# Top-64 routing in the last expert stage: two experts chosen ahead of the weights, and later nodes fetched from DRAM by index

## The chip, the cores and the metric

The kernel runs on one core of a Trainium2 chip. The core has TensorE (PE, with a separate row in the profile for its weight loads, PEld), VectorE (DVE), ScalarE (ACT), GpSimd (POOL) and SyncE (SP), and 16 DMA engines that all its transfers share. SBUF holds the working tiles, PSUM (eight banks here, each 128 x 512 f32) the results of matmuls. The metric is the device time of one execution of the whole program, in microseconds (us); the figure for a kernel is the median over several executions. The data are f32, and a f32 matmul in the source is carried out as two instructions, each with its own weight load; the counts below are of instructions unless they say otherwise.

## The reference

The program is a network of four layers on 512 nodes with 768 features. Each layer adds a graph block and an attention block of the normalized features to `x`, and then a feed-forward block. The change concerns only the feed-forward block of the fourth layer, a mixture of experts in which every *expert* chooses its 64 best nodes:

```python
scores = sigmoid(x @ gate_weight.T)                 # 512 nodes x 16 experts
capacity = ceil(n / E * TOP_K)                      # 512 / 16 * 2 = 64
topk_score, topk_ids = top_k(scores.T, capacity)    # per expert: 64 nodes
xg = x[topk_ids]
gate, up = silu(einsum('ecd,efd->ecf', xg, Wg)), einsum('ecd,efd->ecf', xg, Wu)
out = einsum('ecf,edf->ecd', gate * up, Wd) * topk_score[..., None]
y = zeros((n, d)).at[topk_ids.reshape(-1)].add(out.reshape(-1, d))
return y + silu(x @ Ws_g.T) * (x @ Ws_u.T) @ Ws_d.T # shared expert
```

Here `x` is the layer-normed input, and the result is added to the residual `x`. An expert has a hidden width of 3072; its three matrices are 28.3 MB, those of all sixteen 453 MB. The shared expert has a hidden width of 1536 and sees all nodes.

## The kernel before

**Layout.** Nodes lie in four tiles `t` of 128 (NT = 4, P = 128), features in six chunks of 128 (KC = 6) or two halves of 384 (HW). `xn` is the normalized input with nodes on the partitions, `xnT` the same with features on the partitions. A tile framework lets one write the program in one order; at build time it gives each engine its fixed sequence of instructions, and each instruction its waits on other engines. Nothing is reordered at run time: an instruction that waits holds up all that stands behind it on its engine. PSUM is handed out in banks by `ps` (L222); `copy` (L230) evicts a bank by DVE (L234) and ACT (L236) in turn; `acc` (L310, its matmul is L312) sums products into a bank; `tr` (L317) transposes a block through PE; `to_fm` makes the transposed form of a whole tensor.

**Weights.** `w` (L238) takes one buffer of 128 x 2304 f32 (1152 KB, 1.18 MB) from a pool and has the SP queue load it. In the last stage the pool `f3_w` has ten buffers. SP issues the loads in the order of the program, and each load waits until PE has read the last matmul's operand out of the buffer that it takes over; the loads behind it on SP wait with it. The weights of the shared expert (0.39 MB each) come on POOL's queue into a pool of six.

**Before the stage.** `last_two` (L1398) computes the attention and graph blocks of layer 4. At its end, for each tile `t`, the projection's halves are added to `x` (`add_x`, L360) and `norm1` (L344: statistics L351 and L352, Sqrt on ACT L353, reciprocal L354, the result L355, on DVE) writes the tile of `xn`; after the last tile `to_fm` makes `xnT`, 24 transposes and six copies.

**The seam.** `ffn3` (L1567) first needs its routing:

- *Logits* (L1582 on): for each tile of nodes, the six chunks of `xnT` are the stationary operand and the gate's 16 columns move: 48 matmuls of 16 columns. ACT applies the Sigmoid (L1586) and writes `sc`, nodes by experts.
- *Constants*: two iotas on POOL (L1588, L1590), and `before` (L1593), four 128 x 512 masks by DVE: entry (i, j) of tile t is 1 where node j comes before node 128 t + i.
- *`rank(e)`* (L1597): four transposes of the broadcast column of `sc` put expert e's 512 scores on every partition. For each tile DVE counts the scores that are greater (L1605, 512 columns) and those that are equal and earlier (L1607, 512 columns), each with its sum over the columns; L1609 adds the two. A node's rank is that number, and nodes of rank below 64 are chosen.
- *`choose(g)`* (L1613) compares the ranks of four experts with 0 to 63 (L1616, four instructions of 256 columns): `oh` is one-hot, nodes by slots.
- *`gather(g, f)`*: a matmul of `xn` by `oh` for a chunk f gives the chosen rows of four experts, transposed, in `xg`: 48 instructions of 256 columns for a group of four, and six copies.

Ahead of the first expert matmul stand, in this order on PE, the ranks of experts 0 to 3, `choose(0)`, two matmul pieces of the shared expert (`shared`, L1651; loads L1654, Silu L1661, product L1663), six gathers and the two `shared_down` pieces that belong to them.

**The stream.** Eight pairs q of experts times eight blocks n of 384 hidden units are 64 steps. Step i runs `up` for step i + 1 (L1685: 24 source matmuls in two halves of 64 PE columns, one for each expert of the pair; Silu L1688 on ACT, product L1689 on DVE) and `down` for step i (three transposes, a copy, 12 source matmuls L1701 that accumulate over n in two banks). Its loads are issued as four for `up` of step i + 1 (`up_w`: Wg and Wu of both experts) and two for `down` of step i.

A table `beside` attaches the other work to steps: for g = 1 to 3 the ranks of the next four experts at steps 16(g-1) + 0, 2, 4, 6, `choose(g)` at + 8, the gathers at + 9 to + 14; for each pair, `way` (L1632, one-hot times score, transposed) and four `back` (the outputs of a pair scattered to the nodes by matmul and added to `x`); and the remaining 44 pieces of the shared expert over the first 60 steps. After the last step come four `back` and, for each, the store of a tile of the result by SP (L1758).

An earlier stage already fetches rows by index: a POOL instruction (L828) reads rows of a DRAM copy of the normalized input, `f_there`, into `xb`, and a like DRAM tensor `f_back` is written by ACT's queue.

## Time and profile before

| | us |
|---|---|
| median of three executions (range) | 4346.05 (4344.59 to 4347.77) |
| the profiled execution's own time | 4347.94 |
| its span | 4346.1 |
| PE busy | 4152.7 (96%) |
| PE weight loads | 2128.3 (49%) |
| DVE busy | 1319.1 (30%) |
| ACT busy | 649.5 (15%) |
| POOL busy | 262.9 (6%) |
| mean granted PE clock | 0.984 |
| moved by DMA | 705.98 MB, of it 601.13 MB on SP's weight queue (q1) |

Events in the trace, in us from the start of the span:

| event | us |
|---|---|
| last matmul of the attention projection ends | 3165.7 |
| SP begins to issue the expert weights | 3165.8 |
| last tile of `xn` written | 3169.3 |
| logits begin and end on PE | 3170.4, 3180.2 |
| `sc` written | 3181.8 |
| DVE's ranks of experts 0 to 3 | 3183.1 to 3210.4 |
| gathers on PE | 3210.9 to 3224 |
| first expert matmul (L1685) | 3229.2 |
| first weight load after the first ten is issued | 3233.3 |
| last weight data land | 4331.5 |
| last matmul ends | 4342.1 |

One execution is profiled, so durations come from that one. Busy time is the sum of the durations on an engine, and in this profile the ends of matmuls are modelled: a PE that is busy all the time need not work at its peak. In a row of a group, "busy, mean ns" stands ahead of a bar, and behind it the idle time that the engine had just ahead of these instructions, with what released it. In tables by stretches of time, the number in brackets counts instructions, and the last three columns are the granted PE clock (1 is full), the busy share of the 16 DMA engines and the rate in GB/s.

### The profile page before, as it was taken

Reading aid. Unit: us, or ns where it says so; the run is one execution under the profiler, and the core shown is the slowest. Engines: PE = TensorE matmul, PEld = TensorE weight load, DVE = VectorE, ACT = ScalarE, POOL = GpSimd, SP = SyncE. Lnnn points to the kernel's source line nnn. Section 1 sums busy time; section 2 is a strip of 40 time slices with the busy share of each in tenths; the row PEclk is TensorE's granted clock in tenths of the full one; section 3 lists DMA queues with packets and bytes.
Section 4 is the critical chain, followed back from the end, with each engine's and each line's share of the span. In section 5 each row is a group of like instructions: output and inputs, shape, how many; then the busy total and the mean of one; then the engine's idle time right before and its main releaser. Section 6 shows DMA issues by size and latency. Waiting matters only on the chain. (4 is left out here: it accounts for less than half of the span.)

```text
span 4346.1 us, 40145 instructions
## 1 busy us (share of the span) xinstructions
PE 4152.7 (96%) x16454; PEld 2128.3 (49%) x16454; DVE 1319.1 (30%) x3001; ACT 649.5 (15%) x1235; POOL 262.9 (6%) x307
## 2 busy tenths in 40 slices
PE   7989999999988999999999999988989999999999
PEld 3434555554444566655544444444654444444444
DVE  7772111113332136513221111125842132131111
ACT  1121200002211224411101010013600000000000
POOL 1120000011021010000000000021200000000000
PEclk9999999999999999999999999999989999999999
DMA  3111011121056112211201110072059999999999
GB/s 109 51 61 56 22 44 65 66 73 39 15 211 243 44 51 71 112 38 66 105 33 66 44 66 33 22 288 82 12 220 417 408 419 420 402 420 414 406 409 376
DMA packets 97819, 705.98 MB, mean 162 GB/s; under 512 B 11856, under 2 KB 11920, under 8 KB 28256
## 3 DMA queue, kind: packets, MB, share of 16 engines
q1 hardware_dynamic: 77776, 601.13, 35.0%
q0 software_dynamic: 15952, 91.22, 5.6%
q10 hardware_dynamic: 3904, 11.01, 0.7%
q8 instruction: 133, 2.18, 0.2%
q14 instruction: 54, 0.44, 0.0%
HBM read 682.34 MB, written 20.97 MB: 162 GB/s over the span
## 5 line engine op out<-in xcount | busy, mean ns | idle before, releaser
L1685 PE MATMUL ps<-w,xg 128*64 128x384 f32 x3072 | 569.2, 489 | 3.7 <-DMA w<-in_f_Wu_dram 2.0
L1685 PEld LDWEIGHTS ps<-w,xg 128*64 128x64 f32 x3072 | 233.5, 137 | 296.1 <-issue 273.9
L1356 PE MATMUL ps<-aT,w 128*128 128x512 f32 x864 | 372.3, 592 | 0.0
L1701 PE MATMUL ps<-w,hT 128*64 128x384 f32 x1536 | 326.4, 490 | 3.4 <-DMA w<-in_f_Wd_dram 2.7
L312 PE MATMUL ps<-xnT,w 128*128 128x512 f32 (+1 forms) x732 | 320.9, 595 | 0.2 <-ACT xnT L236 0.2
L1356 PEld LDWEIGHTS ps<-aT,w 128*128 128x128 f32 x864 | 164.2, 190 | 203.6 <-issue 202.3
L360 DVE TENSOR_TENSOR x<-x,ps 128x384 f32<-128x384 f32 x240 | 131.6, 553 | 326.0 <-PE ps L312 256.2
L312 PE MATMUL ps<-w,xnT 128*128 128x384 f32 x672 | 221.7, 486 | 0.2 <-DVE xnT L234 0.2
L312 PEld LDWEIGHTS ps<-xnT,w 128*128 128x128 f32 (+1 forms) x732 | 134.1, 184 | 174.7 <-issue 171.1
L1701 PEld LDWEIGHTS ps<-w,hT 128*64 128x64 f32 x1536 | 133.3, 136 | 168.5 <-issue 146.6
L312 PE MATMUL ps<-w,hT 128*128 128x384 f32 x552 | 187.9, 496 | 8.8 <-ACT hT L850 8.8
L312 PE MATMUL ps<-C,parts 128*128 128x512 bf16 x864 | 188.6, 380 | 2.7 <-DVE inv L1378 2.7
L463 PE MATMUL ps<-ohd,so 128*128 128x512 bf16 x816 | 180.3, 380 | 2.8 <-DVE so L460 2.8
L312 PEld LDWEIGHTS ps<-w,xnT 128*128 128x128 f32 x672 | 127.0, 190 | 88.8 <-issue 4.8
L1366 DVE TENSOR_TENSOR aT<-inv,ps 128x512 f32<-128x512 f32 x72 | 49.5, 687 | 365.6 <-PE ps L312 365.6
L1688 ACT ACTIVATE h<-ps 128x384 f32<-128x384 f32 x64 | 31.4, 491 | 802.5 <-PE ps L1685 802.5
L312 PEld LDWEIGHTS ps<-w,hT 128*128 128x128 f32 x552 | 104.6, 193 | 83.1 <-ACT hT L850 13.4
L1689 DVE TENSOR_TENSOR h<-h,ps 128x384 f32<-128x384 f32 x64 | 35.5, 554 | 348.4 <-PE ps L1685 336.2
L312 PE MATMUL ps<-w,aT 128*128 128x384 f32 (+1 forms) x416 | 139.6, 486 | 0.5 <-DVE aT L234 0.4
L312 PEld LDWEIGHTS <-parts 128*128 128x128 bf16 x864 | 84.8, 98 | 108.1 <-issue 8.8
L312 PE MATMUL ps<-xnT,sw 128*128 128x512 f32 x288 | 136.3, 605 | 0.0
L460 DVE TENSOR_SCALAR so<-io,ind,worth 128x256 bf16<-128x256 int16 x408 | 121.7, 356 | 35.2 <-PE ps L463 35.0
(478 smaller groups left out, 4853.5 us busy)
## 6 DMA issues: line engine op xcount, KB each, us to landing
w<-in_f_Wg_dram SPq DMA_DIRECT2D x128, 1152.0 KB, 12.0
w<-in_f_Wu_dram SPq DMA_DIRECT2D x128, 1152.0 KB, 12.2
w<-in_f_Wd_dram SPq DMA_DIRECT2D x128, 1152.0 KB, 13.2
w<-in_g_w_dram SPq DMA_DIRECT2D x54, 1152.0 KB, 5.1
w<-in_m_wqkv_dram SPq DMA_DIRECT2D x24, 1152.0 KB, 7.2
w<-in_g_t_dram SPq DMA_DIRECT2D x12, 1152.0 KB, 5.4
w<-in_m_wp_dram SPq DMA_DIRECT2D x8, 1152.0 KB, 5.0
ea<-in_edge_attr_dram SPq DMA_DIRECT2D x34, 256.0 KB, 2.7
```

Source lines behind the costliest of these rows:

```text
L312: self.nc.tensor.matmul(out, a, b, start=n == 0, stop=n == len(pairs) - 1)
L360: self.nc.vector.tensor_add(xs, xs, p)
L460: nc.vector.tensor_scalar(so[:, n, :], io[:, h * 256 : (h + 1) * 256], ind[:, 0, j : j + 1], worth[:, n, j : j + 1], OP.is_equal, OP.mult)
L463: nc.tensor.matmul(p, so[:, n, t * P : (t + 1) * P], ohd[:, j, :], start=False, stop=j == (g + 1) * HJ - 1)
L1356: nc.tensor.matmul(outs[nb * 3 + f], w[:, k, f * P : (f + 1) * P], xT[:, k, :], start=first and k == 0, stop=last and k == KC - 1)
L1366: nc.vector.tensor_mul(aT[:, f, :], inv[:, r, :], p)
L1685: nc.tensor.matmul(p[a * 64 : a * 64 + 64, :HW], xg[:, k, e * CAP : (e + 1) * CAP], ws[b][a][:, k, :], start=k == 0, stop=k == KC - 1)
L1688: nc.scalar.activation(h, pg[:, :HW], AF.Silu)
L1689: nc.vector.tensor_mul(h, h, pu[:, :HW])
L1701: nc.tensor.matmul(po[nb][a * 64 : a * 64 + 64, :HW], hT[:, f * P + a * 64 : f * P + a * 64 + 64], wd[a][:, f, nb * HW : (nb + 1) * HW], s ...
```

## The change

Five things change, all in `last_two` and `ffn3`.

1. `last_two` makes a DRAM tensor `f3_there` (512 x 768) and, behind each of the last four `norm1`, has ACT's queue write the tile of `xn` to it. `to_fm` moves from the end of `last_two` into `ffn3`.
2. The set-up in `ffn3` is written ahead of `to_fm` and on POOL; `before` becomes one 128 x 128 mask. A Sigmoid on a constant column is written there too.
3. Logits: the gate's 16 columns are stationary and `xnT` moves, six source matmuls of 512 columns into 16 partitions, then a copy to SBUF and four transposes back to nodes by experts.
4. `rank(e)`: scores in tiles before the node's own are counted with "greater or equal", those in its own and later tiles with "greater", and equality times `before` is needed in the 128 columns of its own tile alone; `tensor_reduce` adds the three counts.
5. Experts are chosen by pairs. Only the pair of the first eight steps is gathered by matmul, and only its two ranks stand ahead of the first expert matmul, with one piece of the shared expert. For each later pair q, `fetch(q)` makes the node number of each slot (`oh` times `number`, a table that holds each node's number in two parts, four source matmuls; a sum and a conversion to an integer on DVE) and has POOL read the 128 rows from `f3_there`; `turn(q)` transposes them (six transposes, two copies). They are attached as ranks at steps 8(q-1) and + 1, `choose` and `fetch` at + 2, `turn` at + 5. The other 47 pieces of the shared expert are spread over the first 60 steps.

```diff
--- before.py
+++ after.py
@@ -1395,10 +1395,11 @@
-    def last_two(self, xn, xnT, out, outT):
+    def last_two(self, xn, xnT, out):
         nc, tc, d = self.nc, self.tc, self.d
+        there = self.dp.tile([N, D], F32, name="f3_there")
         xs = self.chunks(xnT)
@@ -1455,10 +1456,12 @@
                 if over:
                     while len(ready) <= t:
-                        self.norm1(self.x, out, len(ready))
+                        u = len(ready)
+                        self.norm1(self.x, out, u)
+                        nc.scalar.dma_start(there[u * P : (u + 1) * P, :], out[:, u, :])
                         ready.append(t)
             assert over
-        self.to_fm(out, outT)
+        return there
@@ -1564,7 +1567,7 @@
-    def ffn3(self, xn, xnT):
+    def ffn3(self, xn, xnT, there):
@@ -1577,22 +1580,29 @@
             self.cw.close()
             self.wp = c.enter_context(tc.tile_pool(name="f3_w", bufs=10, side="right"))
+            first = self.small.tile([P, 1], F32, name="r3")
+            nc.scalar.activation(first, self.eps, AF.Sigmoid)
+            io = one.tile([P, P], F32, name="io")
+            nc.gpsimd.iota(io, pattern=[[1, P]], base=0, channel_multiplier=0, allow_small_or_imprecise_dtypes=True)
+            number = one.tile([P, NT, 2], F32, name="number")
+            nc.gpsimd.tensor_copy(number, self.number)
+            above = one.tile([P, NT, NX], F32, name="above")
+            counted = one.tile([P, NX, NT, 3], F32, name="counted")
+            nc.gpsimd.memset(counted, 0.0)
+            before = one.tile([P, P], BF16, name="before")
+            nc.gpsimd.tensor_scalar(before, io, self.me, None, OP.is_lt)
+            self.to_fm(xn, xnT)
             gw = self.col("f3_gw", 0, KC * NX).rearrange("p (k e) -> p k e", k=KC)
             p = self.ps()
+            self.acc(p[:NX], [(gw[:, k, :], xnT[:, k, :]) for k in range(KC)])
+            loT = one.tile([NX, N], F32, name="loT")
+            nc.vector.tensor_copy(loT, p[:NX])
+            p = self.ps()
             for t in range(NT):
-                self.acc(p[:, t * NX : (t + 1) * NX],
-                         [(xnT[:, k, t * P : (t + 1) * P], gw[:, k, :]) for k in range(KC)])
+                self.tr(p[:, t * NX : (t + 1) * NX], loT[:, t * P : (t + 1) * P])
             sc = one.tile([P, NT, NX], F32, name="sc")
             nc.scalar.activation(sc, p[:, : NT * NX].rearrange("p (t e) -> p t e", t=NT), AF.Sigmoid)
-            io = one.tile([P, N], F32, name="io")
-            nc.gpsimd.iota(io, pattern=[[1, N]], base=0, channel_multiplier=0, allow_small_or_imprecise_dtypes=True)
-            me = one.tile([P, NT], F32, name="me")
-            nc.gpsimd.iota(me, pattern=[[P, NT]], base=0, channel_multiplier=1, allow_small_or_imprecise_dtypes=True)
-            before = one.tile([P, NT, N], BF16, name="before")
-            for t in range(NT):
-                nc.vector.tensor_scalar(before[:, t, :], io, me[:, t : t + 1], None, OP.is_lt)
-            above = one.tile([P, NT, NX], F32, name="above")
-            equal = one.tile([P, NT, NX], F32, name="equal")
             def rank(e):
@@ -1600,34 +1610,64 @@
                 for t in range(NT):
                     self.tr(p[:, t * P : (t + 1) * P], sc[:, t, e : e + 1].to_broadcast([P, P]))
                 for t in range(NT):
+                    s = sc[:, t, e : e + 1]
+                    for n, (a, b, op) in enumerate(((0, t * P, OP.is_ge), (t * P, N, OP.is_gt))):
+                        if a < b:
+                            junk = one.tile([P, N], F32, name="junk")
+                            nc.vector.tensor_scalar(junk[:, a:b], p[:, a:b], s, None, op, OP.add,
+                                                    accum_out=counted[:, e, t, n : n + 1])
                     junk = one.tile([P, N], F32, name="junk")
-                    s = sc[:, t, e : e + 1]
-                    nc.vector.tensor_scalar(junk, p, s, None, OP.is_gt, OP.add, accum_out=above[:, t, e : e + 1])
-                    junk = one.tile([P, N], F32, name="junk")
-                    nc.vector.scalar_tensor_tensor(junk, p, s, before[:, t, :], OP.is_equal, OP.mult,
-                                                   accum_out=equal[:, t, e : e + 1])
-                nc.vector.tensor_add(above[:, :, e], above[:, :, e], equal[:, :, e])
+                    nc.vector.scalar_tensor_tensor(junk[:, :P], p[:, t * P : (t + 1) * P], s, before, OP.is_equal, OP.mult,
+                                                   accum_out=counted[:, e, t, 2:3])
+                nc.vector.tensor_reduce(above[:, :, e : e + 1], counted[:, e], AX.X, OP.add)
             chosen = {}
-            def choose(g):
-                chosen[g] = two.tile([P, NT, 4, CAP], F32, name="oh"), two.tile([P, KC, 4 * CAP], F32, name="xg")
+            def choose(q):
+                oh = two.tile([P, NT, 2, CAP], F32, name="oh")
+                chosen[q] = oh, two.tile([P, KC, P], F32, name="xg")
                 for t in range(NT):
-                    nc.vector.tensor_tensor(chosen[g][0][:, t], io[:, None, :CAP].to_broadcast([P, 4, CAP]),
-                                            above[:, t, 4 * g : 4 * g + 4, None].to_broadcast([P, 4, CAP]), OP.is_equal)
-            def gather(g, f):
-                oh, xg = chosen[g]
+                    nc.vector.tensor_tensor(oh[:, t], io[:, None, :CAP].to_broadcast([P, 2, CAP]),
+                                            above[:, t, 2 * q : 2 * q + 2, None].to_broadcast([P, 2, CAP]), OP.is_equal)
+            def gather(q):
+                oh, xg = chosen[q]
+                for f in (0, 3):
+                    p = self.ps()
+                    for k in range(3):
+                        self.acc(p[:, k * P : (k + 1) * P],
+                                 [(xn[:, t, (f + k) * P : (f + k + 1) * P], oh[:, t].rearrange("p e s -> p (e s)"))
+                                  for t in range(NT)])
+                    self.copy(xg[:, f : f + 3, :], p[:, :HW].rearrange("p (k n) -> p k n", k=3))
+            rows = {}
+            def fetch(q):
+                oh = chosen[q][0]
                 p = self.ps()
-                self.acc(p[:, : 4 * CAP], [(xn[:, t, f * P : (f + 1) * P], oh[:, t].rearrange("p e s -> p (e s)"))
-                                           for t in range(NT)])
-                self.copy(xg[:, f, :], p[:, : 4 * CAP])
+                self.acc(p[:, :2], [(oh[:, t].rearrange("p e s -> p (e s)"), number[:, t, :]) for t in range(NT)])
+                sums = two.tile([P, 1], F32, name="sums")
+                nc.vector.tensor_reduce(sums, p[:, :2], AX.X, OP.add)
+                who = two.tile([P, 1], I32, name="who")
+                nc.vector.tensor_copy(who, sums)
+                rows[q] = two.tile([P, D], F32, name="rows")
+                nc.gpsimd.indirect_dma_start(out=rows[q], out_offset=None, in_=there,
+                                             in_offset=bass.IndirectOffsetOnAxis(ap=who, axis=0))
+            def turn(q):
+                for f in (0, 3):
+                    p = self.ps()
+                    for k in range(3):
+                        self.tr(p[:, k * P : (k + 1) * P], rows[q][:, (f + k) * P : (f + k + 1) * P])
+                    self.copy(chosen[q][1][:, f : f + 3, :], p[:, :HW].rearrange("p (k n) -> p k n", k=3))
             def way(q):
-                oh = chosen[q // 2][0][:, :, q % 2 * 2 : q % 2 * 2 + 2, :]
+                oh = chosen[q][0]
                 os = two.tile([P, NT, 2, CAP], F32, name="os")
 ...
@@ -1676,13 +1716,12 @@
 ...
                 return [self.wr(d["f3_Wd"][2 * q + a, n]) for a in range(2)]
             def up(q, n, ws):
-                xg = chosen[q // 2][1]
+                xg = chosen[q][1]
                 pg, pu = self.ps(), self.ps()
                 for b, p in ((0, pg), (1, pu)):
                     for k in range(KC):
                         for a in range(2):
-                            e = 2 * (q % 2) + a
-                            nc.tensor.matmul(p[a * 64 : a * 64 + 64, :HW], xg[:, k, e * CAP : (e + 1) * CAP],
+                            nc.tensor.matmul(p[a * 64 : a * 64 + 64, :HW], xg[:, k, a * CAP : (a + 1) * CAP],
                                              ws[b][a][:, k, :], start=k == 0, stop=k == KC - 1)
 ...
@@ -1706,13 +1745,12 @@
             steps = [(q, n) for q in range(8) for n in range(8)]
             beside = {i: [] for i in range(-8, 64)}
-            for g in range(1, 4):
-                i = 16 * (g - 1)
-                for e in range(4):
-                    beside[i + 2 * e].append((rank, 4 * g + e))
-                beside[i + 8].append((choose, g))
-                for f in range(KC):
-                    beside[i + 9 + f].append((gather, g, f))
+            for q in range(1, 8):
+                i = 8 * (q - 1)
+                beside[i].append((rank, 2 * q))
+                beside[i + 1].append((rank, 2 * q + 1))
+                beside[i + 2] += [(choose, q), (fetch, q)]
+                beside[i + 5].append((turn, q))
             for q in range(8):
                 beside[8 * q + 2].append((way, q))
 ...
@@ -1723,21 +1761,15 @@
-            rest = pieces[4:]
+            rest = pieces[1:]
             for k, piece in enumerate(rest):
                 beside[k * 60 // len(rest)] += piece
-            for e in range(4):
+            for e in range(2):
                 rank(e)
+            shared(0, 0)
             choose(0)
-            for piece in pieces[:2]:
-                for fn, *args in piece:
-                    fn(*args)
-            for f in range(KC):
-                gather(0, f)
-            for piece in pieces[2:4]:
-                for fn, *args in piece:
-                    fn(*args)
+            gather(0)
             held = up(*steps[0], up_w(*steps[0]))
@@ -1823,8 +1855,7 @@
         xn = last.tile([P, NT, D], F32, name="xn")
         xnT = last.tile([P, KC, N], F32, name="xnT")
-        net.last_two(xn, xnT, xn, xnT)
-        net.ffn3(xn, xnT)
+        net.ffn3(xn, xnT, net.last_two(xn, xnT, xn))
```

## The prediction

> **What bounds the kernel now.** I began with the page's busy table and slices, which show two regimes (columns: 40 slices of 109 us).
>
> ```profile
> PE   7989999999988999999999999988989999999999
> PEclk9999999999999999999999999999989999999999
> DMA  3111011121056112211201110072059999999999
> GB/s 109 51 61 56 22 44 65 66 73 39 15 211 243 44 51 71 112 38 66 105 33 66 44 66 33 22 288 82 12 220 417 408 419 420 402 420 414 406 409 376
> ```
>
> From slice 31 on the last stage streams 453 MB of expert weights at about 420 GB/s. The DMA engines are full, and so is PE. Next I cut the seam ahead of that stage into stretches of 5 us (busy time and count of each engine, then PE clock, DMA share, GB/s).
>
> ```profile
> core 0: us, PE busy (x) PEld busy (x) DVE busy (x) ACT busy (x) POOL busy (x), PEclk, DMA share, GB/s
> 3190.00:3195.00 5.00, 5.00 (x13) 2.25 (x12) 4.79 (x14) 1.88 (x2) 0.56 (x1) 1.00 1.01 423
> 3195.00:3200.00 5.00, 0.86 (x3) 0.03 (x1) 3.95 (x13) 0.00 (x0) 0.54 (x1) 0.91 0.51 189
> 3200.00:3205.00 5.00, 0.00 (x0) 0.00 (x0) 4.79 (x14) 0.00 (x0) 0.00 (x0) 0.50 0.00 0
> ...
> 3225.00:3230.00 5.00, 5.00 (x20) 2.64 (x20) 4.25 (x8) 0.00 (x0) 0.41 (x1) 1.00 0.01 3
> 3230.00:3235.00 5.00, 5.00 (x34) 2.21 (x32) 0.00 (x0) 0.49 (x1) 0.12 (x1) 1.00 0.44 110
> ```
>
> The first ten weight tiles fill all ten buffers by 3197. Then DMA stands still until the first expert matmuls (3229.2) free two of them; loads resume at 3233.3, data at 3234. DVE is what PE waits for from 3196 to 3211: the ranking. So 36 us of transfer time are lost.
>
> Is the stream after that limited by DMA or by PE? Stretches of 20 us inside it:
>
> ```profile
> 3295.00:3315.00 20.00, 20.00 (x102) 8.76 (x100) 8.76 (x23) 0.97 (x2) 0.54 (x1) 1.00 1.01 420
> 3455.00:3475.00 20.00, 20.00 (x108) 9.92 (x105) 3.33 (x6) 0.86 (x2) 0.00 (x0) 1.00 0.97 374
> 3735.00:3755.00 20.00, 20.00 (x110) 9.16 (x110) 1.80 (x3) 0.86 (x2) 0.54 (x1) 1.00 0.91 345
> 4035.00:4055.00 20.00, 20.00 (x100) 9.60 (x100) 4.02 (x7) 0.86 (x2) 0.54 (x1) 1.00 0.93 357
> ```
>
> Mostly DMA is full at 420, with dips. At 17.2 us a step from 3229 the dips stand at steps 13, 29 and 47; the gathers of `xn` by `oh` are attached to steps 9–14, 25–30 and 41–46. There PE frees buffers too slowly. In the waits (engine and line, releaser: us, times, longest) PE waits for weights hardly at all, and only at the very end:
>
> ```profile
> PEld ps L1701 <- DMA w<-in_f_Wd_dram: 4.3, 3, 1.9
> PEld ps L1685 <- DMA w<-in_f_Wg_dram: 3.0, 2, 2.2
> PEld ps L1685 <- DMA w<-in_f_Wu_dram: 2.5, 2, 1.3
> ```
>
> The chain of waits ends on the last load and 10 us of PE work (start, length):
>
> ```profile
> 4310.32 22.27 DMA w<-in_f_Wd_dram
> 4332.64 4.08 PE ps L1701 x20
> ```
>
> So two streams run level. **DMA:** 374 loads of 1.18 MB and 27 shared ones of 0.39 MB from 3234 are 451.8 MB; at 420 GB/s 1075.7 us; data ends at 4331.5, 1097.5 us later, so the dips cost 22. **PE:** 3229.2 to its last matmul's end at 4342.1 is 1112.9, less 9.8 of waits: 1103.1 of its own.
>
> **What the Trainium skill says.** "TensorE: Matmul & The Clock Gate", Part 1: an idle window of about 3.4 us halves the PE clock, a busy one restores it. The trace agrees: 0.50 at 3171.8–3185.5 and again at 3199.2–3216.2. "TensorEngine Tiling (Array Packing)", Key Properties: "Changing tiling mode (not just tile) drains the TensorE". The trace shows it: each excursion from 64-row tiles to full ones and back costs 0.4 + 0.2 us between weight loads (3576.92 to 3577.65 against a beat of 0.32). "DMA: Bandwidth & Descriptors", Issuing engines are not separate DMA queues: all transfers share 16 engines, so fetched rows cost bandwidth. Same page, Queues, rings and completion order: engines take rings in turn by packets, so fetched rows need not wait out the weight queue; no run here shows that under full load.
>
> **The start, step by step.** Rows of the groups used (instructions, busy us, mean ns):
>
> ```profile
> L312 PE MATMUL ps<-cols,xnT 128*128 128x16 f32 x48 | 9.8, 353 | 0.2 <-DVE xnT L234 0.2
> L1605 DVE TENSOR_SCALAR_CACHE_REDUCE junk<-ps,sc 128x512 f32<-128x512 f32 x16 | 12.0, 749 | 11.9 <-PE ps L317 11.5
> L1607 DVE SCALAR_TENSOR_TENSOR junk<-ps,sc,before 128x512 f32<-128x512 f32 x16 | 12.0, 750 | 0.5
> ```
>
> *`before` leaves DVE for POOL.* Four instructions stood in the last norm; add to `xn` takes 2.64 us undisturbed (the third norm), so 3165.71 + 2.64 = 3168.35 against 3169.28. POOL's small set-up at 3165.6 ends near 3168, needed at 3178.
>
> *`there`.* Four writes on ACT; a like write (`f_back`) issues in 0.33 us. The fourth ends near 3168.7, before ACT's copies at 3168.8: nothing. Without that cover, 0.3. Its 0.39 MB goes into the filling, in place of a shared load.
>
> *Logits.* First matmul 1.11 after the first transpose, 3169.5. Twelve instructions of 512 columns instead of 48 of 16. Bounds: 0.43 us each at full clock (`xnT`,`w` in the projection), 0.86 at half. I take full: PE's idle gap shrinks from 1.7 to 0.8 us and wide matmuls fill the window that dropped the clock. 5.3 gives 3174.8. Then a copy (0.7), four transposes (0.6): 3176.2.
>
> *Sigmoid warm-up.* In the changed order it stands near the program's start, behind the first norm, where ACT idles from 20.5 to 71.2; other functions follow. It removes nothing: the table load (1.28) before the real Sigmoid stays. `sc` to transposes took 1.64: 3177.8. DVE starts at 3178.9 (0.8–1.3 behind).
>
> *Ranks.* A 512-column count starts every 0.79 us, so 0.257 + columns/960. Per tile 640 columns in three instructions (two for the first): 1.18 + 3×1.44 = 5.5, reduce 0.2 (as L1609). Two experts 11.4 (four took 27.3 with a visitor): 3190.3. `oh` halves to 0.29: 3190.6.
>
> *Gather.* 48 instructions of 128 columns; bounds 0.115 (the 65-column attention gather) and 0.23 (half of the cold 0.46). PE idles before, so 5 us cold, the rest warm: 8 us. The two `shared_down` calls (5.3) move behind. **First expert matmul 3198.7, 30.5 earlier**; loads 4.8 later, 3203.5. Range 3196 (warm) to 3206 (logits cold).
>
> **The stream.** *DMA:* seven fetches of 0.39 MB and two shared loads that fell into filling or idle add 3.5 MB: 455.3 MB, 1084.1 us, data ends at 4287.6 plus dips. *PE:* removed 144 gather instructions at 0.216 = 31.1. Added: shared(0,1) 5.2, shared_down 5.2, two ranks' transposes 0.9, 28 `number` matmuls at 0.23 = 6.4, 42 row transposes at 0.11 = 4.6. Net −8.8, excursions alike: 1094.3, ending 4293.0 plus waits. After the last weights 10.6 us of PE follow: DMA's claim is 4298.2. Before, the larger claim (PE's 4332.3) was exceeded by 9.8 through the streams' mutual hold-ups; with PE's peaks gone I take 6.3: 4304.5. The tail of 4.0 is unchanged. Span **4308.5** against 4346.1: −37.6. That execution took 4347.94, the median shown is 4346.05; from it, 4308.5.
>
> *Queues.* POOL issues each fetch (0.95 us as L828) behind shared loads whose buffers PE frees before the `number` matmul: no added wait. Matmuls keep their order, so a late row stalls PE and everything behind. Between `number` and the transposes PE has some 42 us of work; in the earlier stage `xb` reached PE 7.4 us after issue began. DVE's ranks before each fetch have about 3 us to spare at the first one.
>
> **Rivals.** *Only the start gains* (0.17): the dips are not the gathers' and stay at 22 us. For: a dip at 4135 has no gather. Data ends at 4309.6, span 4324. *Cheaper still* (0.08): warm start, fewer hold-ups, about 4300. *Rows late, slower* (0.06): small packets starve beside 9 KB ones. Each us beyond 42 costs 7 in all, so from 42 + 37.6/7 = 47 us to landing it is slower; at 49 about 4357. Against: weight loads land in 12–13 us. *It does not reach the path* (0.02): 4346. *Mine*, 4302–4316: 0.67.
>
> Faster by over 0.2% (9 us, about what can be told from no change) 0.92, within 0.02, slower 0.06. Range 4301–4325 leaves out late rows and half of the best case, and holds the cold clock.
>
> **What would show it.** Idle DMA between filling and resumption near 6 us; first expert matmul 3196–3206; no dips to 350 GB/s in mid-stream; no PE wait on `rows`; PE waits for weights a few us up. PE waiting on `rows` or on `oh`, or a cold clock through the logits, would prove me wrong.

## The result, and the profile after

| | before | after |
|---|---|---|
| median of four executions (range), us | 4346.91 (4344.59 to 4350.74) | 4307.23 (4305.40 to 4315.56) |
| ratio, 95% interval | | 0.9912 (0.9894 to 0.9929) |
| profiled execution: time, span | 4347.94, 4346.1 | 4315.56, 4313.8 |
| PE busy in the span | 4152.7 | 4125.5 |
| moved by DMA, MB | 705.98 | 710.30 |

The time forecast was 4308.5. Two later sets of executions of the same kernel gave ratios of 0.9918 (0.9901 to 0.9934) and 0.9921 (0.9908 to 0.9935).

The execution that was profiled first happens to be the longest of the four after the change. Part of that has nothing to do with the stage. I call P the end of the attention projection: the last short matmul with the bias in the trace's timeline, plus its 0.33 us. PE's instructions up to P are the same in both kernels, in the same order, but P lies at 3165.7 before and at 3168.7 after, and over the fourteen profiles of this study it lies anywhere from 3160.4 to 3168.7. From here on I compare distances from P.

| us | before | after | after, second profile | after, third profile |
|---|---|---|---|---|
| P | 3165.7 | 3168.7 | 3160.4 | 3162.8 |
| P to first expert matmul | 63.5 | 31.9 | 32.8 | 31.8 |
| first expert matmul to end of span | 1116.9 | 1113.2 | 1112.8 | 1111.7 |
| P to end of span | 1180.4 | 1145.1 | 1145.6 | 1143.5 |

So the stage lost 35 to 37 us, 31 to 32 of them ahead of the first expert matmul and 4 to 5 behind it. By the medians of the three sets the gain is 34 to 40 us.

The slices of the page, 40 of 108 us, after the change (busy tenths, and GB/s):

```profile
PE   7989999999988999999999999978989999999998
DMA  3111011111047112211211111063069999999998
GB/s 110 52 62 56 22 44 66 66 55 53 20 178 269 44 63 71 99 52 46 105 43 66 44 56 55 0 255 129 12 257 419 419 420 420 420 417 420 419 421 362
```

The stage's slices, its first and last aside, stand at 417 to 421 GB/s, where before five of them stood at 402 to 414. The seam in stretches of 5 us (busy time and count of PE, PEld, DVE, ACT, POOL, then PE clock, DMA share, GB/s):

```profile
3185.00:3190.00 5.00, 1.99 (x5) 0.57 (x3) 4.64 (x22) 1.88 (x2) 0.61 (x1) 0.99 1.01 428
3190.00:3195.00 5.00, 1.56 (x7) 1.59 (x8) 4.34 (x18) 0.00 (x0) 0.00 (x0) 0.50 1.01 418
3195.00:3200.00 5.00, 5.00 (x39) 5.00 (x38) 0.56 (x1) 0.00 (x0) 0.00 (x0) 0.82 1.01 418
3200.00:3205.00 5.00, 5.00 (x34) 2.50 (x34) 0.00 (x0) 0.77 (x2) 0.00 (x0) 1.00 0.11 44
3205.00:3210.00 5.00, 5.00 (x29) 2.36 (x26) 1.31 (x4) 0.20 (x1) 0.00 (x0) 1.00 0.85 313
```

PE still waits for DVE's ranks, and its clock still falls to half for one stretch, but DMA is busy through all of it: the filling of the ten buffers ends just as the first expert matmuls begin (3200.6), and the next load is issued at 3204.7, when these have freed two. DMA stands still for 4 to 5 us in place of some 36.

The same four stretches inside the stream that were shown of before:

```profile
3295.00:3315.00 20.00, 20.00 (x107) 8.79 (x106) 4.01 (x7) 0.49 (x1) 0.54 (x1) 1.00 1.01 420
3455.00:3475.00 20.00, 20.00 (x95) 8.48 (x92) 1.79 (x3) 0.49 (x1) 0.54 (x1) 1.00 1.01 420
3735.00:3755.00 20.00, 20.00 (x117) 9.52 (x115) 3.33 (x6) 0.49 (x1) 0.00 (x0) 1.00 1.01 420
4035.00:4055.00 20.00, 20.00 (x110) 9.14 (x106) 10.05 (x32) 1.94 (x4) 0.54 (x1) 1.00 1.02 422
```

The dips to 345 to 374 are gone; from 3255 to 4275 no stretch of 20 us stands below 396. The chain of waits still ends on a weight load (start, length):

```profile
4276.19 23.75 DMA w<-in_f_Wd_dram
4299.98 4.08 PE ps L1740 x20
4304.07 5.37 PE ps L312 x16
```

And the rows that are fetched by index are early: what the trace says of the line that issues them ends with the time from issue to landing (least, median, greatest), and names no one who waited.

```profile
L1656 POOL DMA_INDIRECT rows<-f_there,who x7: 997/997/1037, 3240.8 to 4076.8; - x7
...
DMA to landing us min/median/max: 7.3/7.6/8.9
```

### The profile page after: what moved, and what is told of

It reads as the page before. It is cut to its first block, busy times and chain, and to the rows that moved or that the text cites. A ratio compares the mean times of both kernels' runs of the same rounds, so it can differ in the third digit from the quotient of the medians.

```text
span 4313.8 us, 40131 instructions
## 1 busy us (share of the span) xinstructions
PE 4125.5 (96%) x16376; PEld 2099.9 (49%) x16376; DVE 1305.0 (30%) x3120; ACT 650.1 (15%) x1233; POOL 270.3 (6%) x316
## 2 busy tenths in 40 slices
DMA packets 98956, 710.30 MB, mean 165 GB/s; under 512 B 12032, under 2 KB 12097, under 8 KB 29393
## 3 DMA queue, kind: packets, MB, share of 16 engines
q10 hardware_dynamic: 4480, 12.58, 0.8%
```

## The experiments

Each edit is against the changed kernel; line numbers in a profile are those of the kernel that it shows. "P to end" is the distance defined above, from the one profile of each run; the medians and ratios come from the executions beside it, and 4344 to 4346 was the median of before beside them.

| run | P to first expert matmul | P to end | median, us | ratio to before (95%) |
|---|---|---|---|---|
| before | 63.5 | 1180.4 | 4346.91 | 1 |
| changed kernel (three profiles) | 31.8 to 32.8 | 1143.5 to 1145.6 | 4307.2 to 4310.4 | 0.9912 to 0.9921 |
| rows of experts 4 to 15 by matmul | 31.9 | 1172.5 | 4338.00 | 0.9984 (0.9977 to 0.9991) |
| four experts ahead | 51.3 | 1161.7 | 4325.84 | 0.9959 (0.9945 to 0.9973) |
| logits with the gate moving | 35.9 | 1147.0 | 4310.90 | 0.9924 (0.9908 to 0.9941) |
| ranks in full columns | 34.7 | 1146.4 | 4313.05 | 0.9924 (0.9908 to 0.9941) |
| no scatter of seven pairs | 31.8 | 1144.1 | 4308.09 | 0.9915 (0.9898 to 0.9931) |
| shared weights kept | 31.9 | 1142.6 | 4307.15 | 0.9913 (0.9897 to 0.9930) |
| both of these | 31.8 | 1116.2 | 4284.64 | 0.9861 (0.9846 to 0.9877) |
| rows turned at once | 31.9 | 1188.9 | 4358.51 | 1.0031 (1.0020 to 1.0043) |
| more buffers, late warm-up | 31.2 | 1138.9 | 4304.95 | 0.9906 (0.9889 to 0.9922) |
| that, with less PE work | 31.2 | 1138.3 | 4307.05 | 0.9910 (0.9894 to 0.9925) |

**The changed kernel again.** No edit.

> The changed kernel once more, unchanged. Its first profiled execution (span 4313.8) was the longest of four (the others 4303.6 to 4305.7), and it came to the end of the projection 3.0 us later than the execution of the kernel before, in code that the change does not touch. If that and the last loads are chance: span 4303 to 4307, end of the projection at 3164 to 3167, first expert matmul 31.0 to 32.5 after it, last weight data within 1 us at full rate. If they belong to the kernel: span again near 4313, projection at 3168.7.

Measured: median 4307.49, profiled span 4306.0, P at 3160.4 and the first expert matmul 32.8 behind it, both a little outside the ranges. The 8 us between the two profiles lie ahead of P, in code that both share, so the first reading holds; the last loads were not chance, though. In this profile too the rate falls over the last 4 us ahead of the last landing, to 124 and then 18 GB/s (115 and 18 in the first profile), and P to end is the same within half a microsecond. A third set, later and on the same chip as the last experiments:

> The changed kernel unchanged, beside the run before it on the same chip: 4305 to 4309, and 1144 to 1147 from the end of the projection to the end of the span, as in its two profiles so far (1145.1 and 1145.6).

Measured: 4310.41, P to end 1143.5. The distance came out half a microsecond below the range that I had written, the median 1.4 above it.

**The start without the fetched rows.** The stream of before behind the start of after, with experts 2 and 3 gathered by matmuls of their own. `choose4` and `gather4` (not shown) are the `choose` and `gather` of the kernel before, and `oh` has one buffer in place of two:

```diff
-            for q in range(1, 8):
-                i = 8 * (q - 1)
-                beside[i].append((rank, 2 * q))
-                beside[i + 1].append((rank, 2 * q + 1))
-                beside[i + 2] += [(choose, q), (fetch, q)]
-                beside[i + 5].append((turn, q))
+            beside[0].append((rank, 2))
+            beside[1].append((rank, 3))
+            beside[2].append((choose, 1))
+            beside[4].append((gather, 1))
+            for g in range(1, 4):
+                i = 16 * (g - 1)
+                for e in range(4):
+                    beside[i + 2 * e].append((rank, 4 * g + e))
+                beside[i + 8].append((choose4, g))
+                for f in range(KC):
+                    beside[i + 9 + f].append((gather4, g, f))
```

> The new start, but the rows of experts 4 to 15 come by matmul at the old places (three groups, 48 instructions of 256 columns each), those of experts 2 and 3 by 48 of 128. My account (the gathers' PE time makes the dips, the two streams run level): PE's own work grows from 1094.3 by 31.1 + 11.0 and loses 7 x 1.57 for the fetches, 1125.4; from 3198.7 that ends at 4324, with waits and the tail 4328 to 4338, and DMA dips to 340-390 GB/s return at three places. Rival (the dips are not the gathers', only the start gains): no dips beyond those of the changed kernel, 4304 to 4312.

Measured: 4338.00. The start is as good as in the changed kernel (31.9), and yet only 6 to 8 us of its gain are left at the end. Three stretches of 20 us at and behind the places of the gathers, and one between two of them:

```profile
3395.00:3415.00 20.00, 20.00 (x99) 9.45 (x97) 4.43 (x8) 0.86 (x2) 0.00 (x0) 1.00 0.83 320
3755.00:3775.00 20.00, 20.00 (x103) 8.78 (x101) 4.01 (x7) 0.49 (x1) 0.54 (x1) 1.00 0.86 326
4025.00:4045.00 20.00, 20.00 (x95) 8.86 (x96) 1.24 (x2) 0.86 (x2) 0.54 (x1) 1.00 0.86 337
3600.00:3620.00 20.00, 20.00 (x127) 8.87 (x125) 5.53 (x20) 0.97 (x2) 0.00 (x0) 1.00 1.01 421
```

The large dips return with the gathers. Smaller ones stand elsewhere too (362 from 3475 to 3495, behind the first group's last gather, and 371 to 381 from 3565 to 3585, ahead of the second group), which fits PE's work as a whole running late, with the gathers as the largest piece of it: from its first expert matmul to its last one PE is busy for 1127.0 us here and for 1097.3 in the changed kernel. One dip of before had no gather beside it (333 from 4135 to 4145); neither this run nor the changed kernel has it, and what made it was not tested. The rival that the start is all is out. Fetching by index is what makes the start's gain reach the end; by these sums, the pieces of the shared expert that moved into the stream find room there only without the gathers.

**Four experts ahead.** The reverse: later rows by index, but the old amount of work ahead of the first expert matmul.

```diff
-            rest = pieces[1:]
-            for e in range(2):
+            rest = pieces[4:]
+            for e in range(4):
                 rank(e)
-            shared(0, 0)
             choose(0)
-            gather(0)
+            choose(1)
+            for piece in pieces[:2]:
+                for fn, *args in piece:
+                    fn(*args)
+            gather(0)
+            gather(1)
+            for piece in pieces[2:4]:
+                for fn, *args in piece:
+                    fn(*args)
...
-            for q in range(1, 8):
+            for q in range(2, 8):
```

> The changed kernel, but four experts are ranked, chosen and gathered and four pieces of the shared expert are done ahead of the first expert matmul, as before; the later rows still come by index. My account: two more ranks 11.4, a second gather 7 to 11 and two down pieces 5.3 move the first expert matmul by 24 to 27 us and the end by 22 to 26, because DMA sets the end: 4328 to 4334. Rival (the stream has slack and takes a late start up, since PE has less to do in it): 4307 to 4318.

Measured: 4325.84, first expert matmul 19.4 later than in the changed kernel, not 24 to 27. The timeline of PE ahead of the first expert matmul shows what I had added up wrongly (start, busy):

```profile
3175.46 11.29 PE L312 MATMUL ps<-xnT,sw 128*128 128x512 f32 x24
3186.59 5.52 PE L312 MATMUL ps<-oh,xn 128*128 128x128 f32 x48
3198.61 8.38 PE L312 MATMUL ps<-oh,xn 128*128 128x128 f32 x48 [6.50 <-DVE oh L1631]
3206.83 5.33 PE L312 MATMUL ps<-sw,hs 128*128 128x384 f32 x16
```

The first pair's gather runs while DVE ranks the second pair, so it costs nothing. The last gather starts 13.1 later than in the changed kernel (two ranks, and the one-hot, a product and a copy that DVE does between them) and takes 1.2 longer; with the 5.3 of the down pieces that makes the 19. What the start loses arrives: P to end is 16 to 18 longer. The rival that the stream has slack for a late start is out.

**Logits and ranks.** Each of the two smaller parts was put back alone.

```diff
-            self.acc(p[:NX], [(gw[:, k, :], xnT[:, k, :]) for k in range(KC)])
-            loT = one.tile([NX, N], F32, name="loT")
-            nc.vector.tensor_copy(loT, p[:NX])
-            p = self.ps()
             for t in range(NT):
-                self.tr(p[:, t * NX : (t + 1) * NX], loT[:, t * P : (t + 1) * P])
+                self.acc(p[:, t * NX : (t + 1) * NX],
+                         [(xnT[:, k, t * P : (t + 1) * P], gw[:, k, :]) for k in range(KC)])
```

> The changed kernel, but the logits with the gate moving (48 instructions of 16 columns), as before. My account: first logit to scores takes 11.3 us as before in place of 8.2, the clock falls in it, and all of the 3 us reach the end: 4309 to 4312. Rival (the clock that falls also slows the gather, which would otherwise run warm): 5 us or more.

Measured: 4310.90, first expert matmul 3 to 4 later, P to end 1 to 4 longer, according to which of the three profiles of the changed kernel it is compared with. The logits take 9.0 us on PE in place of 5.3, with the clock at half from 3166.9 to 3180.6. I had put the loss at 3 us. The gather takes 8.4 us here against 7.2 in the first profile of the changed kernel, but 8.1 in its second, so the rival (a slower gather) is not shown.

```diff
-                    for n, (a, b, op) in enumerate(((0, t * P, OP.is_ge), (t * P, N, OP.is_gt))):
+                    for n, (a, b, op) in enumerate(((0, 0, OP.is_ge), (0, N, OP.is_gt))):
...
-                    nc.vector.scalar_tensor_tensor(junk[:, :P], p[:, t * P : (t + 1) * P], s, before, OP.is_equal, OP.mult,
+                    nc.vector.scalar_tensor_tensor(junk, p, s, before[:, t, :], OP.is_equal, OP.mult,
```

(The masks of 128 x 512, not shown, are made by DVE again.)

> The changed kernel with ranks in full columns as before (counts and equalities over 512 columns, but with the later count alone: two instructions a tile; the four 128x512 masks made by DVE again). My account: two experts take 13.6 us of DVE in place of 11.4, the masks 0.9 us in the last norm; the first expert matmul stands 34 to 36 us behind the end of the projection in place of 32 to 33, and the end moves by as much, 1147 to 1149 us from the end of the projection to the end of the span. Rival (more DVE work beside the stream holds up the copies that PE waits for): 1152 or more.

Measured: 4313.05, against 4346.44 of before beside it; first expert matmul 2 to 3 later, P to end 1 to 3 longer: as expected for the start, a little less at the end. The intervals of both ratios hold the ratios of the changed kernel: in time alone neither part can be told from nothing here. The traces price them at 3 to 4 and 2 to 3 us of the start.

**Which stream sets the end.** One experiment takes work from PE and no bytes from DMA. It leaves out the scatter of seven of the eight pairs, so that their outputs never reach the result; 56 additions on DVE, which is 30% busy, go with it:

```diff
-                if q < 7:
-                    for t in range(NT):
-                        beside[8 * q + 8 + t].append((back, q, t))
```

> The changed kernel without the scatter of the outputs of the first seven pairs (so the result lacks them): PE loses 112 instructions of 384 columns at 0.32, 36 us, and DMA nothing. My account (data at 420 GB/s now set the end): 4299 to 4307, small dips and hold-ups vanish, PE waits for weights all along, the DMA engines stay full. Rival (PE's own work still sets the end): 4271 to 4280.

Measured: 4308.09. Another takes bytes from DMA alone; the shared expert then uses the weights of its first two blocks throughout:

```diff
                     for n in ("f3_sg", "f3_su", "f3_sd"):
-                        w = sp.tile([P, D], F32, name="sw")
-                        nc.gpsimd.dma_start(w, d[n][u])
-                        hs[u].append(w)
+                        if u < 2:
+                            w = sp.tile([P, D], F32, name="sw")
+                            nc.gpsimd.dma_start(w, d[n][u])
+                            kept[u, n] = w
+                        hs[u].append(kept[u % 2, n])
```

> The changed kernel, but the shared expert's blocks 2 to 11 use again the weights of blocks 0 and 1 (so its result is another): 30 loads of 0.39 MB less, 28 us of data, the same PE work. My account: data end earlier, and PE's own work (1094 from the first expert matmul) becomes the bound at once, so that only 3 to 10 us are gained: 4297 to 4304, and the DMA engines show gaps. Rival (DMA alone is the bound and PE has much to spare): 4279 to 4284.

Measured: 4307.15. Neither 36 us of PE nor 28 us of data is worth anything that can be told from noise by itself; both medians lie above their ranges, by 1 and by 3 us. What they turn into is seen in the waits. Without the scatter (engine and line, releaser: us, times, longest), PE waits for weights in mid-stream:

```profile
PE ps L1724 <- DMA w<-in_f_Wg_dram: 31.5, 22, 2.1
PE ps L1724 <- DMA w<-in_f_Wu_dram: 8.6, 9, 1.2
PE ps L1740 <- DMA w<-in_f_Wd_dram: 6.8, 10, 1.2
```

With kept weights PE waits for weights no more than in the changed kernel, and DMA has gaps instead. Two long stretches of the stream, first without the scatter, then with kept weights:

```profile
3500.00:3700.00 200.00, 191.24 (x980) 87.32 (x976) 37.53 (x106) 11.98 (x24) 5.26 (x8) 0.99 1.01 420
3900.00:4100.00 200.00, 190.91 (x989) 85.89 (x990) 41.15 (x122) 11.48 (x23) 4.71 (x7) 1.00 1.01 420
```

```profile
3500.00:3700.00 200.00, 199.38 (x1016) 90.08 (x1014) 45.47 (x125) 11.98 (x24) 1.89 (x2) 1.00 0.99 405
3900.00:4100.00 200.00, 199.38 (x994) 89.53 (x991) 48.99 (x137) 10.99 (x22) 1.89 (x2) 1.00 1.00 407
```

Each edit alone fits two level streams, but would fit a third limit as well, one that neither touches. So both together:

> The two edits of e5 and e6 together: no scatter of the first seven pairs (36 us of PE) and the shared weights used again (28 us of data); the result is another. Each alone brought nothing. If two level streams explain that: the smaller of the two savings comes out, less the hold-ups, 22 to 30 us: 4278 to 4286. Rival (neither stream is the bound; the end is set by something else, as the pace at which buffers change hands): 4300 to 4307 again.

Measured: 4284.64, P to end 27 to 29 us shorter, 23 to 26 by the medians: nearly the whole of the smaller saving comes out. A third limit within some 23 us is ruled out, and the two streams stand level to 3 us. In this run DMA is at 421 GB/s in the same two long stretches and PE waits 29.7 us for weights, so data set its pace, as they should when 36 us are taken from PE and 28 from them.

The streams are not level at the end, though. In the changed kernel PE is full up to 4254, and then runs ahead of its weights while DMA stays full:

```profile
4255.00:4275.00 20.00, 18.34 (x112) 7.65 (x106) 1.34 (x3) 1.46 (x3) 0.00 (x0) 1.00 1.01 422
4275.00:4295.00 20.00, 15.60 (x83) 6.47 (x84) 1.44 (x3) 0.97 (x2) 0.00 (x0) 1.00 1.01 422
```

All its 7.2 us of waits for weights stand there. The pieces of the shared expert are spread over the first 60 of the 64 steps, so the last steps have the same bytes and less work for PE. With kept weights it is the same (5.3 us of such waits, PE 16.5 of 20 us busy from 4266.6 on, DMA at 421): ten buffers hold 11.8 MB, 28 us of transfer, so what is saved early in the stream can hardly be carried to its end. That is argued, not shown; no run moved pieces of the shared expert into the last four steps.

**Late rows.** The price of the rival that would have made the kernel slower:

```diff
-                beside[i + 2] += [(choose, q), (fetch, q)]
-                beside[i + 5].append((turn, q))
+                beside[i + 2] += [(choose, q), (fetch, q), (turn, q)]
```

> The changed kernel, but the fetched rows are transposed in the step in which they are fetched, not three steps later: between the node numbers and the transposes PE has 4 us of work for a path of about 10 us, so it stalls seven times for 5 to 7 us. My account (PE and DMA run level, so late rows cost their full time, the rival of the prediction that would have made the kernel slower): 35 to 45 us more, 4343 to 4352, and DMA dips behind each stall. Rival (ten buffers hold a lead that swallows a stall of 6 us): 4307 to 4314.

Measured: 4358.51, slower than before. P to end is 44 longer than in the changed kernel. PE's waits for rows are 30.0 us in seven times; around one of them, in stretches of 5 us:

```profile
PE ps L317 <- DMA rows<-f_there,who: 30.0, 7, 4.8
```

```profile
3810.00:3815.00 5.00, 5.00 (x33) 2.73 (x31) 1.95 (x8) 0.97 (x2) 0.00 (x0) 1.00 1.01 418
3815.00:3820.00 5.00, 3.47 (x20) 1.28 (x16) 0.56 (x1) 0.00 (x0) 1.00 (x1) 1.00 1.00 418
3820.00:3825.00 5.00, 2.46 (x5) 1.04 (x6) 0.00 (x0) 0.00 (x0) 0.00 (x0) 0.56 1.02 424
3825.00:3830.00 5.00, 5.00 (x22) 2.64 (x21) 2.27 (x4) 0.48 (x1) 0.00 (x0) 0.76 1.01 420
3830.00:3835.00 5.00, 5.00 (x21) 2.24 (x18) 0.00 (x0) 0.00 (x0) 0.00 (x0) 1.00 0.90 345
```

PE stops for 4.1 to 4.8 us each time, and its clock falls to half (0.56, 0.76): the trace's record of the clock has half speed for 3.4 us with four of the stalls and for 6.8 with three, 34 us in all. Some 6 of these lie in the stalls themselves, since the clock falls 2 to 5 us behind the beginning of a stall; the other 28 ran at half speed, which loses 14. 30 and 14 are 44, as measured from P. By the medians the run is 48 to 51 longer, above the range that I had written. The ten buffers swallow next to nothing: DMA stays full during the stall and drops (345) behind it. So the rival's mechanism is real, and what keeps it away is the distance of three steps between fetch and transposes, 42 us for a path of about 10.

**A better kernel?** The room that the narrower ranks and the smaller `oh` and `xg` leave in SBUF holds an eleventh weight buffer and a seventh shared one; and the warm-up Sigmoid is made to read the last chunk of `xnT`, so that it cannot move to the program's start.

```diff
-            sp = c.enter_context(tc.tile_pool(name="f3_s", bufs=6))
-            self.wp = c.enter_context(tc.tile_pool(name="f3_w", bufs=10, side="right"))
+            sp = c.enter_context(tc.tile_pool(name="f3_s", bufs=7))
+            self.wp = c.enter_context(tc.tile_pool(name="f3_w", bufs=11, side="right"))
-            nc.scalar.activation(first, self.eps, AF.Sigmoid)
             self.to_fm(xn, xnT)
+            nc.scalar.activation(first, xnT[:, KC - 1, :1], AF.Sigmoid)
```

> The changed kernel with eleven weight buffers and seven for the shared expert in the room that the change left, and the warm-up Sigmoid made to wait for the last chunk of the transposed input, so that the table is loaded during the logits. Fills 1.18 + 0.39 MB (3.7 us) of the 4 to 5 us in which DMA stands still, and the scores come 1.3 us earlier. If data set the end: 3 to 5 us faster, 4302 to 4304.5. If PE's own work does: only the 1.3 us of the start, 4306.

Measured: 4304.95, between the two expectations; P to end 1138.9, 5 to 7 us less in the profile. On ACT the table is loaded under the logits, and the Sigmoid that makes the scores starts at once when they are there (timeline, start and busy):

```profile
3173.39 1.28 ACT L1595 ACT_TABLE_LOAD   x1
3174.68 0.20 ACT L1595 ACTIVATE r<-xnT 128x1 f32<-128x1 f32 x1
3179.10 0.22 ACT L1605 ACTIVATE sc<-ps 128x64 f32<-128x64 f32 x1 [4.22 <-issue]
```

The stretch in which DMA moved 44 GB/s moves 302:

```profile
3200.00:3205.00 5.00, 5.00 (x33) 2.15 (x30) 0.00 (x0) 0.86 (x2) 0.00 (x0) 1.00 0.80 302
```

Then PE was relieved as well (`loT` and `counted` only make room for an eighth shared buffer):

```diff
-                oh = two.tile([P, NT, 2, CAP], F32, name="oh")
+                oh = (two.tile([P, NT, 2, CAP], BF16, name="ohb") if q else
+                      two.tile([P, NT, 2, CAP], F32, name="oh", bufs=1))
...
-                [(oh[:, t].rearrange("p e s -> p (e s)"), number[:, t, :]) for t in range(NT)]
+                [(oh[:, t].rearrange("p e s -> p (e s)"), self.number[:, t, :]) for t in range(NT)]
...
-            sp = c.enter_context(tc.tile_pool(name="f3_s", bufs=7))
+            sp = c.enter_context(tc.tile_pool(name="f3_s", bufs=8))
-            loT = one.tile([NX, N], F32, name="loT")
+            loT = two.tile([P, N], F32, name="ohT")[:NX]
-            counted = one.tile([P, NX, NT, 3], F32, name="counted")
+            counted = one.tile([P, 2, NT, 3], F32, name="counted")
```

> The changed kernel with both streams relieved: eleven weight buffers and eight for the shared weights, the warm-up Sigmoid behind the last chunk of the transposed input, and the one-hot of the pairs 1 to 7 in bf16, so that each node-number product is four instructions of one pass in place of eight (0.92 us, 7 times, to about 0.2: 5 us of PE). If level streams are right: e8 gained 6 us from the end of the projection to the end of the span (1138.9 against 1145.3), this takes 3 to 5 more: 1134 to 1136, time 4297 to 4303. Rival (e8's limit is the pace of the buffers, not PE's work): 1138 to 1140, 4302 to 4307.

Measured: 4307.05, P to end 1138.3. The rival's number: less work for PE brought nothing. The traces show where it went. From the first expert matmul to the last one PE is busy for 1091.5 us in place of 1095.4 in the run before it, and idle for 11.2 in place of 8.0: what was saved became waiting. The chain of waits ends on data, as in the changed kernel, with the two loads ahead of the end filling 43.7 us:

```profile
4247.59 21.43 DMA w<-in_f_Wd_dram
4269.08 22.28 DMA w<-in_f_Wd_dram
```

Beside the changed kernel on the same chip it measured 4307.05 against 4310.41, with overlapping intervals of the ratios. In the profiles both variants are 5 to 7 us shorter from P to end; in time neither is shown to be faster than the changed kernel, though both are faster than before.

## Why the prediction was right

**The time.** 4308.5 was forecast, 4307.23 measured. In the profile, the span was 4313.8; with P where it was before (3.0 earlier) it would be 4310.8, so the stage itself is 2.3 longer than forecast (0.7 to 2.8 over the three profiles). Two terms, one too long and one too short, make that up. That the median agrees to 1.3 us is in part luck: the two terms cancel, single executions of this kernel range over 10 us, and one term, the 6.3 us of hold-ups, was chosen and not worked out.

**The start** was worked out at 33.0 from P to the first expert matmul (3198.7 less 3165.7) and is 31.9. PE's side of it (start, busy):

```profile
3168.36 0.33 PE L312 MATMUL ps<-bias,sel 96*128 96x384 bf16 x1
3172.53 5.32 PE L312 MATMUL ps<-xnT,cols 128*16 128x512 f32 x12 [0.24 <-DVE xnT L234]
3180.75 1.09 PE L317 MATMUL ps<-ident,sc 128*128 128x128 f32 x8 [1.64 <-ACT sc L1605]
3193.44 7.18 PE L312 MATMUL ps<-oh,xn 128*128 128x128 f32 x48 [6.45 <-DVE oh L1631]
3200.55 0.87 PE L1724 MATMUL ps<-w,xg 128*64 128x384 f32 x4
```

Step by step, from P: the first transpose of the scores at 12.1 by forecast, 12.1 by the trace; logits 5.3 and 5.3, at full clock; two ranks 11.4 and 11.4 (DVE, 3181.6 to 3193.0); gather 8 and 7.1. The cost of the ranks rests on 960 columns a microsecond; the new counts show that rate: they take 349, 484, 617 and 748 ns for 128, 256, 384 and 512 columns, 133 ns for each 128. The warm-up, which I said would move and remove nothing, did so: the Sigmoid stands at 22.0, and a table load of 1.28 us still stands at 3179.2, ahead of the scores. Data flow again at 36.8 behind P (3205.5); 37.8 was forecast. The half clock that I had put into the first 5 us of the gather lasts from 3190.0 to 3196.8, so 3.4 us of it fall into the gather. The Trainium skill, "TensorE: Matmul & The Clock Gate", Part 1, from which I took that an idle window cools PE, agrees here (PE stood for 6.45 us) and in the late-rows run (4.1 to 4.8). It does not account for the first fall that I had named, 3171.8 before: that one stands 1.4 us behind the first logit, and PE had stood for 1.7 us at most. With the old logits put back into the new start the clock falls 2.2 us behind the first logit, after a stop of 0.8. So by these runs the narrow logits themselves let the clock fall; the wide ones ran at full clock in all three profiles of the changed kernel.

**The dips** were taken to be the gathers' and to vanish. They vanished, and the start without the fetched rows brought them back. The rival at 4324 (start alone, dips stay) had its cause wrong, and its number too: a start alone is worth 6 to 8 us, not 22; by PE's busy times, the shared pieces that it displaces into the stream meet the gathers there.

**The stream** is where a term was mis-sized. From the first data of the resumption to the last data I took 1084.1 us of transfer plus 6.3 of hold-ups, 1090.4. The trace has 1094 (3205.5 to 4299.3). The bytes were right (455.4 MB on the queues of the weights and rows by the trace, 455.3 by the sum), so the hold-ups are 10 us: DMA falls to 313 and 318 GB/s in two stretches of 5 us right behind the resumption, has short dips (343 to 398 over 5 us) near 3826, 4001, 4221 and 4226, and moves 94 GB/s from 4295 to 4300, which alone loses over 3. The slow end was not foreseen, and no run shows its cause. The 9.8 us from which the 6.3 was taken were no measure of hold-ups either: they are the waits that had been subtracted to get PE's 4332.3.

PE's own work came out as forecast. Its busy time from the first expert matmul to the end of the last one is 1105.7 us before and 1097.3 after, 8.4 less, and 8.8 less was the sum. Both levels of the forecast (1103.1 and 1094.3) stand about 3 too low, since the 9.8 that it took off are waits of the weight loads, and PE itself was idle for 7.2. So the gain of the stream was 4 to 5 us and not 7. The tiles that the prediction calls 64-row tiles are 64 columns wide and have 128 rows (`128*64` in the trace).

**Level streams.** The prediction called the streams of before level, and put DMA's claim on the new kernel at 4298.2 and PE's at 4293 plus waits. That is the point the runs bear out most sharply: from P to the end, 36 us off the one or 28 off the other is worth at most 3 us, both together 27 to 29. I did not draw the conclusion in the expectations of those two runs, though, where I still gave each up to 8 or 10 us.

**Rows** land 7.3 to 8.9 us after issue and nobody waits for them, though the DMA engines are full: the weight loads beside them take 14 to 15. So the rows did not starve, as the rival had it. Its price (late rows cost 7 us for each microsecond) was right in kind but too low: 30 us of stall cost 44, more than their own length, because of the clock.

One edit costed at nothing did make something wait. SP's fill waits 6.3 us for a write to `f3_there`, and the last two of the ten loads are issued only at 3180.6. It costs nothing, since eight loads are queued by then and the DMA share stays at 1.01. The four writes are also 1.57 MB in all (12.58 against 11.01 MB on ACT's queue), not the 0.39 MB of one that the prediction put into the filling. The cover that I had named, ACT's idle time, was not the one that was needed.

## What to carry to other kernels

When two streams run level, neither's relief shows by itself: before you drop an idea because it brought nothing, take from both at once. Here a start that was cut short paid in full only where the stream behind it had room for what was moved there. And a fetch that is off the critical path stays off it by distance alone: write down how many microseconds of other work lie between issue and use, and what a miss would cost, the clock included.

## What the runs showed that I had not expected

- A PE that stops for 4 us in mid-stream loses more than the stop: the clock stands at half for 3.4 or 6.8 us from about its end on, so seven stalls of 30 us in all cost 44.
- PE's clock can fall while PE issues matmuls: 48 of 16 columns took 9.0 to 9.8 us, with the clock at half from 1.4 to 2.2 us behind the first one on; twelve of 512 columns did the same work in 5.3 us at full clock.
- Identical code ahead of the stage ended anywhere within 8.3 us (P from 3160.4 to 3168.7). That is nearly as large as the whole spread of the times of this kernel, 10 us, and more than the effect of the two smaller parts of the change. A distance from a mark in the trace separates what the medians cannot.
- From the first profile of the changed kernel to the second, P to end differs by 0.5 us while the spans differ by 7.8. The third is 2.1 shorter than the second, so differences of 2 us are not told apart by this distance either.
